# One chunk in each 12th and 13th group fetched row by row through SP, with other shares for DVE and ACT

## The chip, the cores and the metric

The kernel runs on one core of one Trainium2 chip. The core has five engines that run their own instruction streams: TensorE (PE; its weight loads are shown apart as PEld), VectorE (DVE), ScalarE (ACT), GpSimd (POOL) and SyncE (SP). They are held together by semaphores. Sixteen DMA engines move data between HBM and the on-chip memories; SP issues plain transfers, POOL issues the indirect ones (gathers). PSUM, the memory that PE writes to, is divided into banks. The metric is the time on the device in microseconds (us), as the median of several runs.

## The reference

The model is a layer norm, a two-layer graph network and a residual, over 12,500 nodes of 128 features and 200,000 edges that are sorted by their destination:

```python
h = jnp.maximum(_layernorm(x, axis=-1), 0.0)
deg = segment_sum(ones, dst);  wsum = segment_sum(edge_weight, dst)
w = edge_weight / jnp.maximum(wsum, EPS)[dst]
feat = relu(h @ W_pool + b_pool)
neigh = segment_max(feat[src] * w[:, None], dst)        # 0 where deg is 0
rst = h @ W1_self + neigh @ W1_neigh + b1
h1 = relu(rst / jnp.maximum(norm(rst), EPS))
neigh2 = segment_sum(h1[src] * w[:, None], dst) / jnp.maximum(deg, 1.0)[:, None]
out = x + relu(h1 @ W2_self + neigh2 @ W2_neigh + b2)
```

The costly parts are the two gathers, `feat[src]` and `h1[src]`: 200,000 rows of 512 bytes each, in random order.

## The kernel before

**Groups and chunks.** The edges are taken in 391 groups of 512 (`NG = 391`, `G = 512`); the last has 320. A group has four chunks `j = 0..3` of 128 edges. A gathered chunk is a tile of 128 partitions (edges) by 128 columns (features). Layer 1 goes over all groups with one Python loop over `i`, layer 2 with a second one. Both are written with a manual schedule: the order in which the loop body states the instructions is the order in which each engine runs them. The body of turn `i` works on several groups at once, each in another stage.

**Three ways to fetch a chunk.** Most chunks come by POOL: `gather` (L513) issues one indirect DMA per chunk (L520), which reads 128 rows of the table in HBM (`feat_d` in layer 1, `h_d` in layer 2). Some chunks are left out there (the argument `besides`) and fetched from a copy of the table that lies turned in SBUF (`one_way`, `other_way`: features on partitions, nodes along the columns), where a row is a column. The class `Columns` (L709) does this on DVE, two columns per instruction (`two_by_two`, L797, recorded as L800), or on ACT, one per instruction (`one_by_one`, L790, recorded as L788). For each such chunk SP loads the list of its 128 places (`listed<-at_d`, L738), the engine reads 16 of them at a time into registers (`TENSOR_LOAD`, L742), and copies 16 columns; these eight steps are spread over the turns ahead of the chunk's group. `every` says in each how many groups the engine takes a chunk, `j` says which chunk, `first` which group comes first.

**Layer 1** (loop at L1002; the first `FIRST = 16` groups are computed from `x` itself while the tables are made). Turn `i`: POOL gathers group `i` into a ring of buffers, which is 18 groups long at first and shrinks to 14 and to 8 (`buffer`, L134); ACT scales the four chunks of the group by their edge weights into `gs` (L1035); PE turns group `i-1` into PSUM, `pm` (L1040); DVE runs a segmented running maximum over `pm` (the scan, L1055), and two groups' worth of selection follows: `sel` (L1067, made by DVE, three buffers), `sc` (L1078, L1081), PE's transposes `pr` (L1095), ACT's copy `rows` (L1050), PE's products of `rows` and `sel` (L1104), and ACT's copy of the 48 result columns into the accumulator (L985). Nodes whose edges are all done go through the linear stage `nodes1` in five turns, among them a store of `h` to `h_d` (L886). A chunk from DVE or ACT holds a row of the normalised `x` in layer 1, so PE multiplies it by `W_pool` (L951) and ACT cuts it (L954) to make a row of `feat`.

**Layer 2** (loop at L1216). Turn `i`: POOL gathers group `i` into a ring of eight; DVE makes the weighted places of the group (L1165 and L1169, tile `s`), fetching some columns between the two; PE multiplies the four chunks of group `i-1` by `s` into `pa` (L1175, L1177; three buffers in PSUM); DVE adds `pa` of group `i-2` into the accumulator (L1180). A chunk fetched by columns is turned back by PE into `flip` (L1151, two halves of one tile in one PSUM bank) two turns ahead of its group, and copied into the ring by ACT (L1154, recorded as L788). `nodes2` makes the output rows.

**SP's queue.** SP runs its instructions in order. In layer 1 it loads four groups' keep masks at a time (`kt`, L602, into two buffers), the lists for the columns (L738), and the stores of `h` (L886). In layer 2 it loads lists, rows of `x` (L895), and stores the output (L915). A load that overwrites a buffer waits for that buffer's last reader, and what stands behind it in the queue waits with it.

**POOL's queue** holds almost nothing but the gathers. A gather waits until the ring buffer that it writes has been read: by ACT (L1035) in layer 1, by PE (L1177) in layer 2.

Of the kernel before, what the change touches and what calls it, by code (L numbers as in the profile page):

```python
# [41 lines left out]
TABLES_AT = (16512, 66880)  # L42
BURST = 16
HIGH = 1.0e30
KEPT = 4
# [4 lines left out]
def gnn_kernel(ctx, tc, x, src, dst, ew, w_pool, b_pool, w1s, w1n, b1, w2s, w2n, b2, out):  # L50
# [461 lines left out]

    def gather(gt, table_d, g, only=None, last=None, besides=()):  # L513

        t, r, ne, chunks = edges_of(g)
        limit = {} if last is None else dict(bounds_check=last, oob_is_err=False)
        for j, k in chunks if only is None else chunks[only:only + 1]:
            if any(c.j == j and c.takes(g) for c in besides):
                continue
            nc.gpsimd.indirect_dma_start(  # L520
                out=gt[:k, j, :], out_offset=None, in_=table_d[:, :],
                in_offset=bass.IndirectOffsetOnAxis(ap=srcT[:k, t, j, r:r + 1], axis=0), **limit)
        return gt
# [180 lines left out]
    def pairs_of(g):  # L704

        t, r, ne, _ = edges_of(g)
        return t, r, ne, [(j, min(P, ne // 2 - j * P)) for j in range(-(-ne // (2 * P)))]

    class Columns:  # L709
# [212 lines left out]
    with tc.manual_schedule(), tc.tile_pool(name="ew", bufs=3) as wk, \  # L922
# [15 lines left out]
        for k, engine, copy, j, every, first in (  # L938
                (0, mybir.EngineType.DVE, two_by_two, 1, 6, FIRST + 16),
                (1, mybir.EngineType.Activation, one_by_one, 3, 5.5, FIRST + 12)):  # L940

# [11 lines left out]
            def cut(g, _, k=k, rows_of_chunk=rows_of_chunk):  # L953
# [48 lines left out]
        for i in range(max(turn) + 6):  # L1002
# [11 lines left out]
            if FIRST <= i < NG:  # L1014
                gts[i] = gather(buffer(i, True), feat_d, i, besides=bycol)

# [106 lines left out]
            for c in bycol:  # L1123
                c.turn(i, c.multiplied)
        assert not busy
        i = NG
# [5 lines left out]
    with tc.manual_schedule(), tc.tile_pool(name="ew2", bufs=3) as wk, \  # L1132
            tc.tile_pool(name="ep2", bufs=2, space=PSUM) as ps:
        place = ps.tile([P, 2 * Q, CW], F32, bufs=1)
        hit, iota = place[:, :Q, :], place[:, Q:, :]
        flip = ps.tile([P, 2, P], F32, bufs=1)
        for j in range(Q):
# [5 lines left out]
        for k, engine, copy, j, every, first in (  # L1143
                (0, mybir.EngineType.DVE, two_by_two, 1, 3, 17),
                (1, mybir.EngineType.Activation, one_by_one, 2, 3.5, 12)):

# [3 lines left out]
            def turned(g, _, k=k, slot=slot):  # L1150
                nc.tensor.transpose(flip[:, k], slot(g), ident)  # L1151

            def back(g, _, k=k, slot=slot):
                by_scalar(slot(g), flip[:, k], **({} if k else {"scale": signs}))  # L1154
# [16 lines left out]
        def window_product(g):  # L1171
            chunks = edges_of(g)[3]
            pas[g] = ps.tile([P, LW], F32, name="pa", bufs=3)
            gt, s = gts.pop(g), ss.pop(g)
            nc.tensor.matmul(pas[g], ones_r[0:1, :P], nothing[0:1, :], start=True, stop=False)  # L1175
            for j, k in reversed(chunks):
                nc.tensor.matmul(pas[g][:, SHIFT[j]:SHIFT[j] + CW], gt[:k, j, :], s[:k, j, :], start=False, stop=j == 0)  # L1177

# [37 lines left out]
        for i in range(max(turn) + 2):  # L1216
            for c in bycol:
                c.turn(i, c.load)
            if EARLY <= i < NG:
                gts[i] = gather(buffer(i, False), h_d, i, besides=bycol)  # L1220
                weighted_places(i, lambda: bycol[0].fetch_one(i))
# [18 lines left out]
            if i == NG - 1:  # L1240
                for n in (HI - 2, HI - 1):
                    own[n] = flip[:, 0] if n % 2 else ps.tile([P, Q, D], F32, name="pl", bufs=1)[:, 0]
                    linear_own(own[n], n, "2s")
# [135 lines left out]
```

## Time and profile before

| | |
|---|---|
| median of 3 runs | 3544.11 us (3543.92 to 3545.5) |
| time of the profiled execution | 3545.64 us |
| its span, first to last instruction | 3543.9 us |
| layer 1's scans | 121 to 1844 us |
| layer 2's weighted places | 1871 to 3526 us |
| busy: DVE, ACT, POOL, PE | 3130.4, 3081.4, 2619.8, 2211.6 us |
| gathers by POOL in layer 1, in layer 2 | 1373, 1330 |
| instructions L788 on ACT, L800 on DVE | 21,376 columns and 233 copies; 11,840 pairs |
| SP: transfers issued in the column lists' line L738 | 359 |

How the lines of the profile are read: a row of the busiest groups gives line, engine, operation, `output<-inputs` and the count; behind the bar the time in which at least one of them ran and the mean duration in ns of one; behind the second bar the idle time of the engine just before them and what ended it. Where instructions overlap, as they do on DVE and ACT, the mean duration is longer than the time that each adds. "Issue" is idle time in which the engine waited for nothing that the profile shows. A row of waits says who waited (engine, tile, line), for whom, for how long in total, how often and the longest time. A timeline row begins with start and length in us; a last bracket holds the idle time ahead. A row of a stage table gives the stretch in us from the start, its length, and the busy time and count of the engine (of all engines in the order PE, PEld, DVE, ACT, POOL where there are five pairs), then the granted clock of PE, the share of the DMA engines and GB/s. A row of a line's instructions gives the duration in ns as minimum, median and maximum; engines with a `q` are their queues: register reads, semaphore waits and DMA issues, which are not counted as busy.

### The profile page before, as it was taken

To read this page: it belongs to the slowest core of one execution; us is meant where nothing else is said; L and a number is where in the kernel's file an instruction comes from. 1 tells how busy PE (TensorE), PEld (TensorE's weight loads), DVE (VectorE), ACT (ScalarE), POOL (GpSimd) and SP (SyncE) were. 2 spreads that over 40 slices of the span, in tenths; PEclk is the share of its full clock that TensorE was granted. 3 is DMA by queue.
4 is the path that set the end of the run, shared out by engine and by line. 5 is a ranking of instruction groups with operands and counts; after the bars stand their busy time and mean duration, and the time that the engine had idled before them with its cause. 6 is when DMAs were issued, how large, how long until landed. Compare 5 with 4: busy or idle time off the path is not lost.

```text
span 3543.9 us, 71968 instructions
## 1 busy us (share of the span) xinstructions
PE 2211.6 (62%) x9504; PEld 1920.0 (54%) x9504; DVE 3130.4 (88%) x16737; ACT 3081.4 (87%) x25633; POOL 2619.8 (74%) x2784
## 2 busy tenths in 40 slices
PE   7666666666666666566565667565565556556556
PEld 6455555555656555555554555555455555455545
DVE  7799999999999999998866888888888888888887
ACT  6689999999999999898967888888888888888885
POOL 6577777777777777777777777777777777777774
PEclk8665555555555555555555555555555555555555
DMA  6433332333333333332222222222222222222221
GB/s 223 130 97 90 94 88 83 88 86 88 86 87 86 88 86 88 86 88 86 83 82 54 54 60 75 60 63 63 60 60 63 63 60 62 63 59 59 62 62 49
DMA packets 132987, 280.13 MB, mean 79 GB/s; under 512 B 49446, under 2 KB 58764, under 8 KB 132494
## 3 DMA queue, kind: packets, MB, share of 16 engines
q0 software_dynamic: 88544, 181.42, 20.2%
q1 hardware_dynamic: 43214, 93.11, 7.8%
q14 instruction: 414, 3.39, 0.3%
q8 instruction: 79, 1.29, 0.2%
q10 hardware_dynamic: 736, 0.92, 0.1%
HBM read 253.41 MB, written 21.87 MB: 78 GB/s over the span
## 4 chain that ended last, share of the span: by engine, by line
DVE 49%; ACT 16%; issue 12%; POOL 6%; PE 6%; DVEq 5%; DMA 4%; ACTq 1%; POOLq 0%
DVE gt L800 25%; ACT gt L788 7%; POOL gt L520 6%; DVE pm L1055 6%; DVE picked L800 5%; DVEq L742 5%; ACT gs L1035 4%; DMA gt<-feat_d,srcT 3%; PE pa L1177 2%; DVE sel L1067 2%; DVE s L1169 2%; PE pf L625 2%; DVE sc L1078 2%; DVE place L1165 1%; ACT rows L1050 1%
## 5 line engine op out<-in xcount | busy, mean ns | idle before, releaser
L788 ACT ACTIVATE gt<-way 128x1 f32 x21376 | 2125.3, 189 | 226.8 <-PE pa L1177 164.5
L520 POOL DMA_INDIRECT gt<-h_d,srcT x1318 | 1246.1, 945 | 411.5 <-issue 340.8
L520 POOL DMA_INDIRECT gt<-feat_d,srcT x1192 | 1127.5, 946 | 369.2 <-issue 302.0
L800 DVE SCALAR_TENSOR_TENSOR gt<-b,way 128x2 f32<-128x2 f32 x8000 | 1155.1, 215 | 182.7 <-issue 154.3
L1177 PE MATMUL pa<-s,gt 128*128 128x24 f32 x3102 | 736.5, 390 | 535.0 <-DVE s L1169 462.4
L1177 PEld LDWEIGHTS pa<-s,gt 128*128 128x128 f32 x3102 | 690.6, 327 | 573.4 <-DVE s L1169 502.8
L1040 PE MATMUL pm<-ident,gs 128*128 128x128 f32 x1499 | 393.5, 415 | 257.9 <-ACT gs L1035 232.1
L800 DVE SCALAR_TENSOR_TENSOR picked<-b,way 128x2 f32<-128x2 f32 x3840 | 541.7, 211 | 1.9 <-issue 1.7
L1055 DVE TENSOR_TENSOR_SCAN pm<-kt,carry,pm 128x512 f32<-128x512 bf16 x389 | 496.3, 1276 | 46.0 <-PE pm L1040 45.8
L1035 ACT ACTIVATE gs<-gt,ewT 128x128 f32<-128x128 f32 x1303 | 414.9, 390 | 73.6 <-DMA gt<-feat_d,srcT 60.1
L1104 PEld LDWEIGHTS pn<-sel,rows 128*128 128x128 f32 x1564 | 354.3, 313 | 170.5 <-ACT way L985 73.2
L1040 PEld LDWEIGHTS pm<-ident,gs 128*128 128x128 f32 x1499 | 283.9, 221 | 294.3 <-ACT gs L1035 276.6
L1104 PE MATMUL pn<-sel,rows 128*128 128x48 f32 x1564 | 356.9, 374 | 135.1 <-ACT way L985 58.6
L1067 DVE TENSOR_SCALAR sel<-cols,lastT,invT 128x48 f32<-128x48 f32 x782 | 245.7, 314 | 0.0
L1095 PE MATMUL pr<-ident,sc 128*128 128x128 f32 x782 | 235.9, 403 | 3.4 <-DVE r_first L291 2.4
L1081 DVE COPY_PREDICATED sc<-kt,pm 128x256 f32<-128x256 int16 x389 | 167.1, 430 | 0.0
L1095 PEld LDWEIGHTS pr<-ident,sc 128*128 128x128 f32 x782 | 164.5, 220 | 4.2 <-ACT gs L1035 3.7
L1078 DVE COPY sc<-pm 128x256 f32<-128x256 f32 x391 | 159.7, 408 | 3.8 <-PE pr L1095 3.7
L1050 ACT ACTIVATE rows<-pr 128x256 f32<-128x256 f32 x392 | 142.1, 363 | 5.3 <-PE pn L1104 5.2
L851 PE MATMUL pn<-w_2n,way 128*128 128x128 f32 x192 | 79.2, 515 | 102.2 <-DVE way L1180 102.2
L1165 DVE TENSOR_TENSOR place<-place,locT 128x96 f32<-128x96 f32 x391 | 100.8, 258 | 46.1 <-DVE way L1180 32.2
L520 POOL DMA_INDIRECT w2T<-feat_d,srcT x96 | 90.8, 946 | 51.9 <-issue 24.1
(303 smaller groups left out, 2735.1 us busy)
## 6 DMA issues: line engine op xcount, KB each, us to landing
kt<-keep_d SPq DMA_DIRECT2D x97, 512.0 KB
gt<-h_d,srcT POOLq DMA_INDIRECT x1318
gt<-feat_d,srcT POOLq DMA_INDIRECT x1192
feat_d<-fr SPq DMA_DIRECT2D x24, 256.0 KB
xr<-in_x SPq DMA_DIRECT2D x24, 256.0 KB
out<-o SPq DMA_DIRECT2D x24, 256.0 KB
h_d<-h SPq DMA_DIRECT2D x47, 128.0 KB
listed<-at_d SPq DMA_DIRECT2D x359, 0.5 KB
```

Source lines behind the costliest of these rows:

```text
L520: nc.gpsimd.indirect_dma_start(out=gt[:k, j, :], out_offset=None, in_=table_d[:, :], in_offset=bass.IndirectOffsetOnAxis(ap=srcT[:k, t, j, ...
L788: nc.scalar.activation(out, in_, AF.Copy, **scale)
L800: nc.vector.scalar_tensor_tensor(slot[:, r + e:r + e + 2], zero_high, columns_read[e], columns_read[e + 1].to_broadcast([P, 2]), op0=OP.su ...
L1035: nc.scalar.activation(gss[i][:k, j, :], gt[:k, j, :], AF.Copy, scale=ewT[:k, t, j, r:r + 1])
L1040: nc.tensor.transpose(pms[i - 1][:, j * P:j * P + k], gs[:k, j, :], ident[:k, :k])
L1050: nc.scalar.activation(rws[g][:k, j, :], pr[:k, j, :], AF.Copy)
L1055: nc.vector.tensor_tensor_scan(pm[:, :ne], kt[:, :ne], pm[:, :ne], carry, op0=OP.add, op1=OP.max)
L1067: nc.vector.tensor_scalar(part, cols[:k, 1, :], lastT[:k, t, j, r:r + 1], invT[:k, t, j, r:r + 1], op0=OP.is_equal, op1=OP.mult)
L1078: nc.vector.tensor_copy(sc[:, :ne // 2], two[:, :, 1])
L1095: nc.tensor.transpose(prs[g][:k, j, :], sc[:, j * P:j * P + k], ident)
L1104: nc.tensor.matmul(pas[g], rows[:k, j, :], sel[:k, j, :], start=j == 0, stop=j == len(chunks) - 1)
L1177: nc.tensor.matmul(pas[g][:, SHIFT[j]:SHIFT[j] + CW], gt[:k, j, :], s[:k, j, :], start=False, stop=j == 0)
```

## The change

A third way to fetch a chunk is added, the class `Rows`: SP copies the 128 rows of a chunk one by one from the table in HBM into a tile `ga` (two buffers), 512 bytes each, with the source taken from a register. It takes chunk 0 of each 12th group in layer 1 (from group 40 to below group 383) and of each 13th in layer 2 (from 26 to below 390). `gather` leaves these chunks out.

For such a chunk SP loads the 128 source numbers from `src` (turn `g - every - 3`), DVE shifts them left by nine bits, which makes byte offsets of them (one turn later), and in eight steps spread over the turns `g - every - 1` to `g - 3` SP reads 16 of them into registers and issues 16 transfers. All 128 add to one semaphore of the chunk. In layer 1 ACT waits for it ahead of its last scaling instruction of the group, in layer 2 PE waits for it ahead of its last product.

Further: the shares of DVE and ACT are set anew (layer 1: DVE in each 6.5 groups instead of 6, ACT in each 6 instead of 5.5; layer 2: DVE in each 3.25 instead of 3, ACT in each 3.25 instead of 3.5). The two halves of `flip` become two tiles in a PSUM bank each; `pa` has two buffers instead of three, and `sel` in layer 1 has two instead of three. In layer 2's turn, the transposes `turned` are stated ahead of ACT's fetch and of the copies `back` instead of behind them. The lists lie in a second row of the tile that holds `bases`.

```diff
-    bases = const.tile([1, NT * P], I32)
+    bases_and_rows = const.tile([2 * 32, NT * P], I32)
+    bases, row_lists = bases_and_rows[0:1, :], bases_and_rows[32:33, :]
...
-            if any(c.j == j and c.takes(g) for c in besides):
+            if j == 0 and byrow and byrow.takes(g) or any(c.j == j and c.takes(g) for c in besides):
                 continue
...
+    class Rows:
+
+        def __init__(self, pool, table_d, every, first, end):
...
+            for g in range(first, end, every):
+                for s in range(P // BURST):
+                    turn = g - every - 1 + s * every // (P // BURST)
+                    self.plan.setdefault(turn, []).append((g, s * BURST))
...
+        def turn(self, i):
+            g = i + self.every + 3
+            if self.takes(g):
+                nc.sync.dma_start(self.list_of(g), src[None, g * G:g * G + P])
+            g = i + self.every + 2
+            if self.takes(g):
+                nc.vector.tensor_scalar(self.list_of(g), self.list_of(g), ROW_SHIFT, None, op0=OP.logical_shift_left)
+
+        def rows(self, i):
+            for g, r in self.plan.get(i, ()):
+                if g not in self.tiles:
+                    self.tiles[g] = self.pool.tile([P, D], F32, name="ga", bufs=2)
+                to = self.tiles[g].bitcast(U8)
+                _, at = nc.values_load_multi_w_load_instructions(
+                    self.list_of(g)[:, r:r + BURST], [mybir.EngineType.SP], min_val=0, max_val=(N - 1) << ROW_SHIFT,
...
+                for k in range(BURST):
+                    row = nc.sync.dma_start(to[r + k:r + k + 1, :], self.bytes[None, bass.ds(at[k], 4 * D)])
+                    row.then_inc(self.sem(g), 16)
...
+        def tile(self, g, engine):
+            n = (g - self.first) // self.every // len(self.sems) + 1
+            came = engine.wait_ge(self.sem(g), 16 * P * n)
...
-                (0, mybir.EngineType.DVE, two_by_two, 1, 6, FIRST + 16),
-                (1, mybir.EngineType.Activation, one_by_one, 3, 5.5, FIRST + 12)):
+                (0, mybir.EngineType.DVE, two_by_two, 1, 6.5, FIRST + 16),
+                (1, mybir.EngineType.Activation, one_by_one, 3, 6, FIRST + 12)):
...
+        byrow = Rows(wk, feat_d, 12, FIRST + 24, NG - 8)
...
-                    nc.scalar.activation(gss[i][:k, j, :], gt[:k, j, :], AF.Copy, scale=ewT[:k, t, j, r:r + 1])
+                    rows_j = byrow.tile(i, nc.scalar) if j == 0 and byrow.takes(i) else gt[:k, j, :]
+                    nc.scalar.activation(gss[i][:k, j, :], rows_j, AF.Copy, scale=ewT[:k, t, j, r:r + 1])
...
-                sel = sels[due(3)] = wk.tile([P, Q // 2, LW], F32, name="sel")
+                sel = sels[due(3)] = wk.tile([P, Q // 2, LW], F32, name="sel", bufs=2)
...
+            byrow.turn(i)
+            byrow.rows(i)
...
-        flip = ps.tile([P, 2, P], F32, bufs=1)
+        flips = [ps.tile([P, P], F32, name=f"flip{k}", bufs=1) for k in range(2)]
...
-                (0, mybir.EngineType.DVE, two_by_two, 1, 3, 17),
-                (1, mybir.EngineType.Activation, one_by_one, 2, 3.5, 12)):
+                (0, mybir.EngineType.DVE, two_by_two, 1, 3.25, 17),
+                (1, mybir.EngineType.Activation, one_by_one, 2, 3.25, 12)):
...
+        byrow = Rows(wk, h_d, 13, 26, NG - 1)
...
-            pas[g] = ps.tile([P, LW], F32, name="pa", bufs=3)
+            pas[g] = ps.tile([P, LW], F32, name="pa", bufs=2)
...
-                nc.tensor.matmul(pas[g][:, SHIFT[j]:SHIFT[j] + CW], gt[:k, j, :], s[:k, j, :], start=False, stop=j == 0)
+                rows_j = byrow.tile(g, nc.tensor) if j == 0 and byrow.takes(g) else gt[:k, j, :]
+                nc.tensor.matmul(pas[g][:, SHIFT[j]:SHIFT[j] + CW], rows_j, s[:k, j, :], start=False, stop=j == 0)
...
+            for c in bycol:
+                c.turn(i, c.turned)
             by_one.fetch_one(i)
             for c in bycol:
                 c.turn(i, c.back)
-            for c in bycol:
-                c.turn(i, c.turned)
             by_one.ahead()
             by_one.fetch_rest(i)
+            byrow.turn(i)
+            byrow.rows(i)
```

More of the change, by code (lines that the diff above doesn't have):

```diff
@@ L43 @@
 BURST = 16
+ROW_SHIFT = 9
 HIGH = 1.0e30
@@ L511, in edges_of, with gather @@
         return *divmod(g, P), ne, [(j, min(P, ne - j * P)) for j in range(-(-ne // P))]
-    def gather(gt, table_d, g, only=None, last=None, besides=()):
+    def gather(gt, table_d, g, only=None, last=None, besides=(), byrow=None):
         t, r, ne, chunks = edges_of(g)
@@ L707, in pairs_of, with takes, list_of, key @@
         return t, r, ne, [(j, min(P, ne // 2 - j * P)) for j in range(-(-ne // (2 * P)))]
+    class Rows:
+        def __init__(self, pool, table_d, every, first, end):
+            self.pool, self.every, self.first, self.end = pool, every, first, end
+            self.name = f"rows{every}"
+            self.sems = [tc.alloc_semaphore(f"{self.name}_{k}") for k in range(4)]
+            self.bytes = table_d[:, :].bitcast(U8).rearrange("n b -> (n b)")
+            self.tiles, self.plan = {}, {}
+            assert first > every + 4
+            for g in range(first, end, every):
+                for s in range(P // BURST):
+                    turn = g - every - 1 + s * every // (P // BURST)
+                    self.plan.setdefault(turn, []).append((g, s * BURST))
+        def takes(self, g):
+            return (g - self.first) % self.every == 0 and self.first <= g < self.end
+        def list_of(self, g):
+            k = (g - self.first) // self.every % 2 * P
+            return row_lists[:, k:k + P]
+        def turn(self, i):
[12 more added lines that the diff above has]
+                    self.list_of(g)[:, r:r + BURST], [mybir.EngineType.SP], min_val=0, max_val=(N - 1) << ROW_SHIFT,
+                    skip_runtime_bounds_check_because="sources of edges are nodes, as the gathers have it")
+                for k in range(BURST):
+                    row = nc.sync.dma_start(to[r + k:r + k + 1, :], self.bytes[None, bass.ds(at[k], 4 * D)])
+                    row.then_inc(self.sem(g), 16)
+                    tc.no_tile_sem_insts.add(row.ins.name)
+                    tc.add_to_no_dep_group(self.key(g), row.ins)
+        def key(self, g):
+            return f"{self.name}_{g}"
+        def sem(self, g):
+            return self.sems[(g - self.first) // self.every % len(self.sems)]
+        def tile(self, g, engine):
+            n = (g - self.first) // self.every // len(self.sems) + 1
+            came = engine.wait_ge(self.sem(g), 16 * P * n)
+            tc.declare_fence(came.ins, group=self.key(g))
+            return self.tiles.pop(g)
@@ L1014, in gnn_kernel @@
             if FIRST <= i < NG:
-                gts[i] = gather(buffer(i, True), feat_d, i, besides=bycol)
+                gts[i] = gather(buffer(i, True), feat_d, i, besides=bycol, byrow=byrow)
             if i < FIRST:
@@ L1150, in turned @@
             def turned(g, _, k=k, slot=slot):
-                nc.tensor.transpose(flip[:, k], slot(g), ident)
+                nc.tensor.transpose(flips[k], slot(g), ident)
             def back(g, _, k=k, slot=slot):
-                by_scalar(slot(g), flip[:, k], **({} if k else {"scale": signs}))
+                by_scalar(slot(g), flips[k], **({} if k else {"scale": signs}))
             bycol.append(Columns(engine, copy, None, other_way, 1, lists_of(k), slot,
@@ L1219, in gnn_kernel @@
             if EARLY <= i < NG:
-                gts[i] = gather(buffer(i, False), h_d, i, besides=bycol)
+                gts[i] = gather(buffer(i, False), h_d, i, besides=bycol, byrow=byrow)
                 weighted_places(i, lambda: bycol[0].fetch_one(i))
@@ L1241, in gnn_kernel @@
                 for n in (HI - 2, HI - 1):
-                    own[n] = flip[:, 0] if n % 2 else ps.tile([P, Q, D], F32, name="pl", bufs=1)[:, 0]
+                    own[n] = flips[0] if n % 2 else ps.tile([P, Q, D], F32, name="pl", bufs=1)[:, 0]
                     linear_own(own[n], n, "2s")
```

## The prediction

> **What bounds the kernel now.** I read the page first: its span, the busy shares, and the chain that ended last.
>
> ```profile
> span 3543.9 us, 71968 instructions
> ...
> PE 2211.6 (62%) x9504; PEld 1920.0 (54%) x9504; DVE 3130.4 (88%) x16737; ACT 3081.4 (87%) x25633; POOL 2619.8 (74%) x2784
> ...
> DVE 49%; ACT 16%; issue 12%; POOL 6%; PE 6%; DVEq 5%; DMA 4%; ACTq 1%; POOLq 0%
> ```
>
> By these lines DVE leads and POOL has a quarter of its time left. A stretch of POOL's timeline says otherwise:
>
> ```profile
> 2599.56 0.94 POOL L520 DMA_INDIRECT gt<-h_d,srcT  x1 [0.30 <-issue]
> 2600.80 0.94 POOL L520 DMA_INDIRECT gt<-h_d,srcT  x1 [0.30 <-issue]
> 2602.05 0.95 POOL L520 DMA_INDIRECT gt<-h_d,srcT  x1 [0.30 <-issue]
> ```
>
> A gather is shown busy for 0.94 us and the next follows after 0.30 us of its own issuing, so POOL spends 1.25 us on each and is full at a shown 76%. The stage tables come next. The first fence has all engines; then come POOL's gathers (L520), the scans (L1055, one per group of layer 1) and the weighted places (L1169, one per group of layer 2), in the same stretches; count in brackets.
>
> ```profile
> 240.00:1340.00 1100.00, 701.92 (x3188) 624.35 (x3188) 1076.18 (x4603) 1050.98 (x7756) 827.26 (x876) 0.55 0.31 88
> 1340.00:1840.00 500.00, 305.90 (x1353) 272.93 (x1352) 450.07 (x1947) 434.92 (x3208) 377.28 (x398) 0.53 0.30 84
> 2080.00:2780.00 700.00, 427.72 (x1759) 366.40 (x1759) 594.56 (x4031) 606.91 (x6015) 529.37 (x561) 0.50 0.24 63
> 2780.00:3480.00 700.00, 416.65 (x1731) 358.56 (x1730) 593.91 (x4032) 604.96 (x5992) 522.66 (x554) 0.50 0.23 61
> ```
> ```profile
> 240.00:1340.00 1100.00, 827.26 (x876) 0.55 0.31 88
> 1340.00:1840.00 500.00, 377.28 (x398) 0.53 0.30 84
> 2080.00:2780.00 700.00, 529.37 (x561) 0.50 0.24 63
> 2780.00:3480.00 700.00, 522.66 (x554) 0.50 0.23 61
> ```
> ```profile
> 240.00:1340.00 1100.00, 321.58 (x252) 0.55 0.31 88
> 1340.00:1840.00 500.00, 140.05 (x110) 0.53 0.30 84
> ```
> ```profile
> 2080.00:2780.00 700.00, 39.68 (x161) 0.50 0.24 63
> 2780.00:3480.00 700.00, 39.93 (x162) 0.50 0.23 61
> ```
>
> Layer 1 until 1340 us: a group takes 1100/252 = 4.365 us and DVE is busy 98% of it. A group needs 4 - 1/6 - 1/5.5 = 3.652 gathers, so 252 groups use up 920 while POOL issues 876: the store of chunks gathered ahead shrinks by 44. From 1340 on it is gone: 500/110 = 4.545 us a group, which is 3.652 x 1.25. POOL issues without a pause throughout, so its count of gathers sets the end of layer 1.
>
> Layer 2 needs 4 - 1/3 - 1/3.5 = 3.381 gathers a group, 544 for the 161 groups of the first half; POOL issues 561 and gains a lead of 17, until the ring of eight buffers is full. So POOL is not the bound there. A group takes 1400/323 = 4.334 us. The waits of DVE and ACT from 2080 to 3480:
>
> ```profile
> DVE gt L800 <- issue: 132.1, 457, 1.3
> DVE place L1165 <- DVE way L1180: 27.6, 71, 1.0
> ```
> ```profile
> ACT gt L788 <- PE pa L1177: 126.6, 55, 6.3
> ACT gt L788 <- issue: 32.9, 96, 0.8
> ACT gt L788 <- PE flip L1151: 21.6, 15, 3.1
> ```
>
> DVE is busy 1188.5 of 1400 us, and 160 us more are waits for its own list reads and results: 96%, with nobody else named. DVE bounds layer 2. ACT is busy 1211.9 us and waits 126.6 us for a ring buffer to be free, which is real slack: it is about 9% away from being the bound.
>
> **The change, part by part.** Counted from the two loops' bounds, layer 1 goes from 60 to 56 chunks by DVE and from 66 to 61 by ACT, and 29 come by SP: 20 gathers fewer. Layer 2 goes from 125 to 115 by DVE, from 108 to 117 by ACT, and 28 by SP: 27 gathers fewer. ACT thus fetches nine chunks more in layer 2 and four more in all. The prices of a chunk:
>
> ```profile
> L788 ACT ACTIVATE gt<-way 128x1 f32 x21376 | 2125.3, 189 | 226.8 <-PE pa L1177 164.5 <-issue 53.1 <-DMA gt<-h_d,srcT 1.5
> ...
> L800 DVE SCALAR_TENSOR_TENSOR gt<-b,way 128x2 f32<-128x2 f32 x8000 | 1155.1, 215 | 182.7 <-issue 154.3 <-PE pa L1177 5.4
> ...
> L800 DVE SCALAR_TENSOR_TENSOR picked<-b,way 128x2 f32<-128x2 f32 x3840 | 541.7, 211 | 1.9 <-issue 1.7
> ...
> L788 ACT ACTIVATE gt<-flip 128x128 f32<-128x128 f32 x108 | 28.0, 259 | 18.6 <-PE flip L1151 18.3
> ```
>
> These instructions overlap, so busy time over count is the price. ACT: 2125.3/21376 = 99.4 ns, 12.7 us for 128 columns, 13.3 us with the copy back and its issue gaps. DVE in layer 2: (1155.1 + 182.7)/125 = 10.7 us; in layer 1: 543.6/60 = 9.1 us.
>
> *Layer 1.* POOL: 20 x 1.25 = 25 us less. DVE: 4 x 9.1 = 36 us less, and 29 shifts of a list more, each on one partition, taken at the 0.21 us of a column pair: 6 us. ACT: 5 x 13 = 65 us less. Both give up more than POOL, so POOL keeps setting the end: -25 us. I keep back 5 us, because ACT now also waits for SP's tile, at a time when it has no lead to live on: **-20 us**, between -25 and 0.
>
> *Layer 2*, a group, in steady state. DVE: 4.334 - (1/3 - 1/3.25) x 10.7 = 4.06, with shifts 4.07 us. POOL: (52 - 4 - 4 - 1)/13 x 1.25 = 4.135 us. ACT: without the wait for PE pa it works 4.334 x (1 - 126.6/1400) = 3.94 us; added are (1/3.25 - 1/3.5) x 13.3 = 0.29 us: 4.23 us. If the wait for PE flip goes as well, since the two turned tiles then no longer share a bank, 0.07 us less: 4.16 us. So the bound passes from DVE to ACT, with POOL beside it. I take 4.20, the middle: (4.334 - 4.20) x 323 groups = **-43 us**. Bounds: POOL's 27 x 1.25 = 34 us plus about 15 us of lead that is used up, -49; and 0, should ACT lose its gain to waits.
>
> *Two pools made smaller.* `sel` goes from three to two buffers and `pa` likewise. With two `pa`, PE may begin group x only after DVE has added x-2, which stands a fetch of eight column pairs (8 x 0.144 = 1.2 us) behind the weighted places that PE waits for now; PE is busy 61% there and a group's product is needed two turns later: nothing. With two `sel`, DVE waits where PE's product of two groups before is late. What can make it late is PE's own wait:
>
> ```profile
> L1104 PEld LDWEIGHTS pn<-sel,rows 128*128 128x128 f32 x1564 | 354.3, 313 | 170.5 <-ACT way L985 73.2 <-DVE r L865 49.0 <-ACT way L890 46.2
> ```
>
> At most the 119 us held by ACT could reach DVE; below nothing is excluded, since a wait gives no time back. DVE has 36 - 6 us of new room and before the end of layer 1 the 50 us that it idles after 1340, so I take 0. The reordering of `turned` and `back` changes no engine's own order: 0.
>
> *SP's new work* is what decides. Each chunk is 8 list reads and 128 transfers of 512 bytes, in a queue that also issues `kt`, the columns' lists and the stores. Its prices:
>
> ```profile
> L738 SPq DMA_DIRECT2D listed<-at_d x359: 214/215/313, 198.6 to 3494.4; - x180
> ```
> ```profile
> L602 SPq DMA_DIRECT2D kt<-keep_d x98: 319/342/435, 117.8 to 1823.9; - x98
> ```
> ```profile
> 336.50 0.53 SPq L738 DMA_DIRECT2D listed<-at_d  x2
> ```
> ```profile
> L742 ACTq TENSOR_LOAD <-listed x1392: 1002/1019/1431, 206.6 to 3503.2; - x199
> ```
>
> The list transfer also moves one run of 512 bytes into one partition: 0.215 us, two of them in 0.53 us, so 0.265 each with the step to the next. A row's source comes from a register, which no row shows; it cannot be cheaper than 0.265. The upper bound is the largest form, `kt`, 0.342 + 0.05 = 0.39 us. I take 0.285, near the lower end, since size and shape are the list's. A read of 16 registers is 1.02 us on ACT; SP's is taken alike. A chunk costs SP 128 x 0.285 + 8 x 1.02 + about 3.2 for three `kt`, four lists and stores = 47.9 us in layer 1, and 48.0 in layer 2 (eight lists, no `kt`). There is room for 12 x 4.365 = 52.4 us and 13 x 4.20 = 54.6 us: SP would be 91% and 88% full, hidden. The covers end at 0.320 us a row in layer 1 and 0.337 in layer 2. Beyond, each 10 ns more costs 29 x 1.28 + 28 x 1.28 = 73 us, for SP is then the pace: ACT stands at the wait for SP's rows (in layer 2 PE), behind it the column fetches and window copies, and DVE stands at the shift of a list that SP sends late. On SP itself, `kt` and the columns' lists queue behind the rows. At 0.342 us a row the sum is -20 + 82 - 43 + 18 = +37 us; at 0.39 it is -20 + 260 - 43 + 190 = +387 us.
>
> [...]
>
> Transfers: 7,296 rows of 512 bytes are 3.7 MB beside 280 MB, with the transfer engines 23 to 31% busy: 0.
>
> **Sum.** -20 - 43 = -63 us against the profiled execution's 3545.6 us (span 3543.9 and 1.7 around it), 3482.6; the median of the runs is 1.5 us below that execution, so **3482 us** is forecast.
>
> **Rivals.**
> *SP has no time for it* (slower). For it: the room is 35 ns a row, and SP is in order; it loses its lead at each wait:
>
> ```profile
> SPq L738 <- DVEq L742: 1202.0, 141, 14.4
> SPq L602 <- DVE r L865: 659.8, 44, 17.9
> ```
>
> Against it: the same rows show SP long idle ahead of the others, and a row is planned three turns before its use. It decides from 0.337 us a row (sum zero). At 0.342 us: 3581 us; at 0.39: 3931 us; at twice the list's duration, 0.43 us, over 4200 us, to which I give 0.03 of this case's chance. [...]
> *The smaller pools give DVE waits* in layer 1: about half of the 119 us arrives, more than DVE's new room, and layer 1 gains nothing; PE delayed in layer 2 takes 10 us more: 3482 + 20 + 10 = 3512 us. For it: layer 1 runs DVE at 98%. Against it: ACT gives up 65 us there, and PE waits for ACT.
> *ACT spoils layer 2*: at 4.33 us a group, full and with every remaining wait on the path, layer 2 stays as it is: 3525 us. For it: 4.23 of 4.334 us is 98%. Against it: its waits are a ring's, and shrink as it falls behind.
> That the edit does not do what it says is excluded: the instruction order has 47 gathers, 896 column pairs on DVE and the matching lists less, and 512 columns on ACT more.
>
> **Chances and range.** My forecast 0.52; SP short 0.30; smaller pools 0.09; ACT 0.09. Within 0.2% (7 us, about what a measurement of this kernel can tell from no change) fall 0.02 of SP's case and 0.02 of the pools'; slower 0.28 of SP's and 0.01 of the pools'. That leaves faster 0.67, same 0.04, slower 0.29. The fast cases lie from 3470 (-25 and -49) to 3537 and hold 0.67; with the same ones and SP up to 0.35 us a row (+95, 3640) it is 0.8. So the range is 3466 to 3640; my forecast's own is 3466 to 3505.
>
> **What would show it.** POOL's gathers: 2,720 instead of 2,767 and still 1.25 us apart in layer 1. SP: rows 0.29 us apart, in bursts of 16, SP waiting for DVE between them. In layer 2 about 4.2 us a group, ACT without its wait for PE pa, POOL's lead not growing. The prediction is wrong if a row takes over 0.32 us start to start, if ACT or PE is seen waiting for SP's rows, or DVE at the shift or at `sel`.

## The result and the profile after

The changed kernel is slower. It takes 3654.6 us (median of four runs, 3652.3 to 3656.2) against 3544.3 us of the kernel before, a ratio of 1.031 with a 95% interval of 1.0295 to 1.0321. The forecast was 3482 us, range 3466 to 3640. The profiled execution took 3653.2 us, span 3651.5.

The page of the changed kernel: its span, the busy shares, and the chain that ended last by engine.

```profile
span 3651.5 us, 86331 instructions
...
PE 2204.4 (60%) x9476; PEld 1922.3 (53%) x9476; DVE 3024.5 (83%) x15898; ACT 3124.8 (86%) x26135; POOL 2573.3 (70%) x2737
...
DVE 37%; SPq 28%; issue 10%; ACT 8%; DVEq 5%; PE 5%; DMA 4%; POOL 2%; ACTq 1%; POOLq 0%
```

DVE's work fell by 106 us, as meant, and yet the span grew. What is new is SPq, SyncE's queue: it wasn't in the chain of before, and now holds 28% of it. The same stretches by stage, all engines first (columns as in the prediction), then the scans of layer 1 (L1114) and the weighted places of layer 2 (L1231):

```profile
240.00:1340.00 1100.00, 665.86 (x2964) 594.79 (x2964) 989.96 (x4108) 941.47 (x6808) 779.16 (x826) 0.52 0.28 83
...
2140.00:2840.00 700.00, 415.21 (x1723) 359.08 (x1724) 544.81 (x3676) 634.64 (x6332) 510.85 (x542) 0.50 0.22 63
```
```profile
240.00:1340.00 1100.00, 300.87 (x236) 0.52 0.28 83
```
```profile
2140.00:2840.00 700.00, 39.27 (x159) 0.50 0.22 63
```

In layer 1 DVE goes from 98% to 90% busy, and POOL from 876 gathers to 826; in layer 2 ACT is the busiest, with 91%. None of the five sets the pace: at 1.25 us a gather POOL has work for 94% of the first stretch and 97% of the second. A group takes 1100/236 = 4.66 us (before 4.365), so twelve groups take 55.9 us. In layer 2 a group takes 700/159 = 4.40 us (before 4.334), thirteen 57.2 us. Both are about the same length: that of one chunk of rows on SyncE. What SyncE does there, by its timeline (start, length, what):

```profile
1000.41 5.09 SPq L749 DMA_DIRECT2D ga<-feat_d  x16
1005.55 0.37 SPq L943 DMA_DIRECT2D h_d<-h  x1
1006.01 0.23 SPq L795 DMA_DIRECT2D listed<-at_d  x1
1006.35 0.34 SPq L604 DMA_DIRECT2D kt<-keep_d  x1
1006.78 0.23 SPq L795 DMA_DIRECT2D listed<-at_d  x1
1008.40 5.16 SPq L749 DMA_DIRECT2D ga<-feat_d  x16
1013.91 0.23 SPq L735 DMA_DIRECT2D bases_and_rows<-in_src  x1
1015.53 11.57 SPq L749 DMA_DIRECT2D ga<-feat_d  x32
1027.22 0.35 SPq L604 DMA_DIRECT2D kt<-keep_d  x1
```

It works almost without a break: the gaps of 1.3 to 1.4 us ahead of each burst are register reads, which this view leaves out, and from 300 to 1300 us all other gaps over 0.1 us add up to 9.5 us. The two lines by themselves (shortest, median and longest in ns):

```profile
L749 SPq MOVE ga<-feat_d x3712: 29/29/38, 229.3 to 1868.0; - x196
L749 SPq DMA_DIRECT2D ga<-feat_d x3712: 224/228/307, 229.4 to 1868.1; - x196
...
L745 SPq TENSOR_LOAD <-bases_and_rows x456: 973/1232/1797, 228.1 to 3582.2; - x152
```

So a row is two instructions, a MOVE of the register and the transfer: 16 in 5.09 us, 0.32 us from one to the next, and 0.332 us in the mean of all from 300 to 1300 us. A read takes 1.24 us in the mean and 1.30 with the step to the next. A chunk needs 128 x 0.332 + 8 x 1.30 + 3.2 (the prediction's figure for the rest) = 56.1 us. SyncE's waits were 1202.0 and 659.8 us in the prediction's two rows; here the largest for the same two issues (lists and `kt`) are:

```profile
SPq L795 <- ACTq L799: 27.7, 13, 24.1
SPq L604 <- DVE r L922: 27.7, 3, 14.3
```

The others stand behind it. Of the lists for the columns, the view of their line in SyncE's queue (L795) says who waited for them, for how long in us and how often. Before, nobody waited for them (L738); now it is 307 us in all:

```profile
who waited for it (us, times):
  DVE s L1231: 132.2, 27
  ACT gs L1094: 62.3, 15
  DVE picked L857: 43.6, 12
  ACT gt L845: 42.4, 8
  DVE sel L1126: 26.4, 6
```

The view of all waits has the first of these rows as "issue" (132.2 us too). It also has ACT waiting for the rows, and DVE at the shift:

```profile
ACT gs L1094 <- ACTq L762: 36.4, 26, 2.5
...
DVE bases_and_rows L738 <- DMA bases_and_rows<-in_src: 33.8, 15, 5.4
```

### The profile page after: what moved, and what is told of

Read it like the earlier page. It is cut to its first block, busy times and chain, and to the rows that moved or that the text cites. A ratio compares the mean times of both kernels' runs of the same rounds, so it can differ in the third digit from the quotient of the medians.

```text
span 3651.5 us, 86331 instructions
## 1 busy us (share of the span) xinstructions
PE 2204.4 (60%) x9476; PEld 1922.3 (53%) x9476; DVE 3024.5 (83%) x15898; ACT 3124.8 (86%) x26135; POOL 2573.3 (70%) x2737
## 4 chain that ended last, share of the span: by engine, by line
DVE 37%; SPq 28%; issue 10%; ACT 8%; DVEq 5%; PE 5%; DMA 4%; POOL 2%; ACTq 1%; POOLq 0%
SPq L749 21%; DVE picked L857 8%; DVE pm L1114 8%; DVE gt L857 7%; ACT gt L845 6%; SPq L745 6%; DVEq L799 5%; DVE sel L1126 3%; DVE sc L1137 2%; DMA listed<-at_d 2%; DVE sc L1140 2%; POOL gt L522 2%; PE pf L627 1%; ACTq L799 1%; PE pa L1240 1%
## 5 line engine op out<-in xcount | busy, mean ns | idle before, releaser
L845 ACT ACTIVATE gt<-way 128x1 f32 x22016 | 2187.9, 189 | 63.3 <-PE pa L1240 27.6
L522 POOL DMA_INDIRECT gt<-h_d,srcT x1291 | 1219.7, 945 | 465.8 <-issue 316.5
L522 POOL DMA_INDIRECT gt<-feat_d,srcT x1171 | 1106.7, 945 | 450.1 <-issue 300.8
L857 DVE SCALAR_TENSOR_TENSOR gt<-b,way 128x2 f32<-128x2 f32 x7360 | 1060.9, 215 | 165.9 <-issue 128.3
L1240 PEld LDWEIGHTS pa<-s,gt 128*128 128x128 f32 x3046 | 681.2, 327 | 614.6 <-issue 498.7
L857 DVE SCALAR_TENSOR_TENSOR picked<-b,way 128x2 f32<-128x2 f32 x3584 | 507.0, 212 | 63.3 <-issue 63.1
L1094 ACT ACTIVATE gs<-gt,ewT 128x128 f32<-128x128 f32 x1276 | 407.3, 390 | 142.3 <-issue 68.6
L1114 DVE TENSOR_TENSOR_SCAN pm<-kt,carry,pm 128x512 f32<-128x512 bf16 x389 | 496.2, 1276 | 4.4 <-DMA kt<-keep_d 2.4
L1237 PE MATMUL pa<-nothing,ones_r 1*128 1x48 bf16 x391 | 78.9, 202 | 513.2 <-DVE way L1243 506.0
L1231 DVE TENSOR_TENSOR s<-place,w2T 128x96 f32<-128x96 f32 x391 | 97.0, 248 | 134.3 <-issue 132.2
```

The source lines that it names most:

```text
L522: nc.gpsimd.indirect_dma_start(out=gt[:k, j, :], out_offset=None, in_=table_d[:, :], in_offset=bass.IndirectOffsetOnAxis(ap=srcT[:k, t, j, ...
L845: nc.scalar.activation(out, in_, AF.Copy, **scale)
L857: nc.vector.scalar_tensor_tensor(slot[:, r + e:r + e + 2], zero_high, columns_read[e], columns_read[e + 1].to_broadcast([P, 2]), op0=OP.su ...
L1094: nc.scalar.activation(gss[i][:k, j, :], rows_j, AF.Copy, scale=ewT[:k, t, j, r:r + 1])
L1114: nc.vector.tensor_tensor_scan(pm[:, :ne], kt[:, :ne], pm[:, :ne], carry, op0=OP.add, op1=OP.max)
L1240: nc.tensor.matmul(pas[g][:, SHIFT[j]:SHIFT[j] + CW], rows_j, s[:k, j, :], start=False, stop=j == 0)
```

## The experiments

Call SyncE's time for one chunk of rows its need, and the time of the groups among which one such chunk falls its room (in layer 1 twelve groups). Theory A: the need exceeds the room and is the pace. Theory B: something else in the change, the smaller pools above all, costs the time. On some chips the kernel before itself takes about 5000 us instead of 3544 us, so every run is compared only with the kernel before on its own chip; e8 to e10, e17 and e18 ran where it takes 3545 us, all others where it takes about 5000 us.

### The first seven, where the kernel before takes 5000 us

```diff
 e1, e5: every 14th and 15th group
-byrow = Rows(wk, feat_d, 12, FIRST + 24, NG - 8)
+byrow = Rows(wk, feat_d, 14, FIRST + 24, NG - 8)
-byrow = Rows(wk, h_d, 13, 26, NG - 1)
+byrow = Rows(wk, h_d, 15, 26, NG - 1)
 e2: no rows, old shares (6 and 5.5 in layer 1, 3 and 3.5 in layer 2)
+byrow = Rows(wk, feat_d, 12, NG, NG)
+byrow = Rows(wk, h_d, 13, NG, NG)
 e3: no register reads, rows from fixed places
-self.bytes[None, bass.ds(at[k], 4 * D)]
+self.bytes[None, 4 * D * (r + k):4 * D * (r + k + 1)]
 e4: one transfer for two rows
+for k in range(0, BURST, 2): dma_start(to[r + k:r + k + 2, :], ...bass.ds(at[k], 8 * D)...)
 e6: the changed kernel itself
 e7: every 20th and 21st group
```

> SP takes a chunk in each 14th group of layer 1 and each 15th of layer 2, all else as in the changed kernel. Theory A (SP's own time is the pace: 128 rows of 0.332 us, 8 register reads of 1.30 us and 3.2 us of other transfers, 56.1 us a chunk): 14 groups of 4.38 us and 15 of 4.22 us leave 61 and 63 us, so SP is hidden and the time falls from 3654 to about 3490 us (3475 to 3510), with POOL's gathers 1.25 us apart in layer 1. Theory B (the pools with two buffers, or ACT's share in layer 2, hold the kernel up, and SP is only slow beside them): the time stays above 3600 us.

> No rows by SP and the shares of DVE and ACT of the kernel before; what is left of the change is sel and pa with two buffers, the two turned tiles in a bank each, and the transposes stated earlier. Theory A: the same as before within 0.3% (3535 to 3555 us). Theory B: 30 to 110 us slower than before, with DVE waiting at sel or PE's delay behind pa passed on.

> The changed kernel with SP's rows taken from fixed places (rows 0 to 127 of the table) and without the register reads, so the fetched chunk is the wrong one. Theory A: a row costs what the lists' transfer did, about 0.27 us, no read of 1.30 us stands between the bursts, a chunk is 38 us on SP and hidden: about 3482 us (3470 to 3500), the time that the prediction gave. Theory B: above 3600 us.

> The changed kernel with half as many transfers by SP: each moves two neighbouring rows of the table (1,024 bytes), so every second row of the chunk is the wrong one; the register reads stay. Theory A: 64 x 0.34 + 10.4 + 3.2 = 35 us a chunk, hidden: about 3485 us (3470 to 3500). If instead the register reads alone held SP up (8 of 1.30 us in a row of waits), it stays above 3560 us. Theory B: above 3600 us.

> The kernel with SP's chunk in each 14th and 15th group once more. In the first series ACT lost over 1,100 us to issuing its own instructions on that chip, in the kernel before as in all others (before took 5002 us there), so that nothing of SP's pace could be read from the times. On a chip where the kernel before takes about 3544 us, theory A gives 3490 us (3475 to 3510), theory B above 3600 us.

> The changed kernel itself on the experiments' chip, beside the kernel before. There a burst of 16 rows takes SP about 9 us instead of 5.1, and the kernel with SP's chunk in each 14th and 15th group is 3.4% slower than before. Theory A (SP's own time is the pace): the time goes with SP's number of chunks, 57 against 50, so 57/50 of the time that 50 chunks take, less what the other engines hold up beside: 5500 to 5850 us. Theory B (another part of the change is the cause): within 2% of the 5170 us of the kernel with 50 chunks.

> SP takes a chunk in each 20th group of layer 1 and each 21st of layer 2 (35 chunks). On the experiments' chip 20 groups take about 120 us and a chunk costs SP about 90 us, so theory A has SP hidden: within 1% of the 4990 to 5017 us of the kernels with cheaper rows, that is at the time of the kernel before. On a chip where the kernel before takes 3544 us: about 3495 us. Theory B: 3% slower than before or more, as with 50 chunks.

Measured, with the end of layer 1 (last scan) and the time from there to the last weighted places:

| kernel | us | ratio, 95% interval | layer 1 ends | layer 2 |
|---|---|---|---|---|
| e1 | 5175.5 | 1.034 [1.0319, 1.0361] | 2581 | 2574 |
| e5 (as e1) | 5167.2 | 1.0345 [1.0322, 1.0369] | | |
| e2 | 5038.0 | 1.0076 [1.0050, 1.0102] | 2528 | 2491 |
| e3 | 5017.1 | 1.003 [1.0017, 1.0042] | 2487 | 2508 |
| e4 | 4991.8 | 0.9978 [0.9967, 0.9988] | 2487 | 2484 |
| e6 | 5347.1 | 1.0686 [1.0650, 1.0722] | 2760 | 2562 |
| e7 | 5068.9 | 1.0121 [1.0081, 1.0160] | 2507 | 2549 |

Most of the expectations were for paces that don't hold there, and missed: e1 isn't hidden, e2 is 0.8% slower than the kernel before instead of the same within 0.3%, e6 lies between its two ranges, e7 is 1% above its own. SyncE's timeline of e6 shows part of why: the same 16 rows take 5.7 to 11.8 us in this stretch.

```profile
1005.18 11.83 SPq L749 DMA_DIRECT2D ga<-feat_d  x16
...
1018.80 19.09 SPq L749 DMA_DIRECT2D ga<-feat_d  x32
...
1040.35 5.69 SPq L749 DMA_DIRECT2D ga<-feat_d  x16
```

The engines lose time in the same way. In e2, ACT's column copies wait 1344.5 us for nothing but their own issue:

```profile
ACT gt L845 <- issue: 1344.5, 2261, 1.9
PEld pa L1240 <- ACT gt L845: 1192.2, 168, 16.7
```

ACT thus bounds layer 2 there, and the nine chunks more that the change gives it can bring no gain. What still follows: theory B is worth 0.8% there (e2, interval 0.5 to 1.0%), and the end of layer 1 moves with SyncE's load: 2760, 2581 and 2507 us with 29, 25 and 18 chunks of register rows, and 2487 us with 29 cheaper ones, 40 us before e2. This is for A. Layer 2 doesn't follow the load there: it takes 2562 us with 28 chunks of register rows (e6), 2574 with 25 (e1) and 2549 with 18 (e7), against 2491 with none (e2). Why stays open. Whether the engines' gain exists where the forecast was made, these runs can't say.

### e8, e9 and e10: the same two kernels where the kernel before takes 3545 us

e8 is the kernel of e1, e9 that of e3, e10 the kernel before.

> The same kernel as in e1: rows in each 14th group of layer 1 and each 15th of layer 2, all else as changed. Theory A (SyncE's own time for the rows is the pace of the changed kernel): a chunk needs 56.1 us of SyncE by the changed kernel's rows, the room is 14 x 4.37 = 61 us and 15 x 4.20 = 63 us, so the engines' gain comes back: 3480 to 3510 us where the kernel before takes 3544 us. Where the kernel before takes about 5000 us, as in e1, 5165 to 5180 us again. Theory B (the smaller pools, the separate turned tiles or ScalarE's larger share make it slower): 3560 us or more where the kernel before takes 3544 us.

> The same kernel as in e3: all rows of the change are fetched, but from fixed places, without register reads (the output is that of other rows). Theory A: a chunk then needs 128 x 0.301 + 3.2 = 41.7 us of SyncE, room 52.4 and 54.6 us, so 3475 to 3500 us where the kernel before takes 3544 us, and about 5015 us where it takes 5000 us. Theory B: as slow as the changed kernel, 3620 us or more, where the kernel before takes 3544 us.

> The kernel before itself, for its profile on the chip of these runs. If it takes about 5000 us there, ScalarE's steps of issue should be the longest idle entry of its waits, with some 0.7 us for instructions that take 0.1 us to start in the profile at 3544 us; the two layers would end near 2520 and 5000 us. If it takes 3544 us, the profile is that of before.

e8 took 3478.6 us, 0.9815 [0.9799, 0.9831]; e9 3467.2 us, 0.978 [0.9764, 0.9797]; e10 3543.4 us. Theory B is out there: both keep the smaller pools, the separate turned tiles and ScalarE's larger share, and gain 67 and 78 us. e8, which fetches the rows of its own lists, is faster than the kernel before and the changed one. In e9 the row is one instruction:

```profile
L746 SPq DMA_DIRECT2D ga<-feat_d x3712: 214/252/391, 215.3 to 1748.1; - x196
```

With the step to the next it is 0.299 us (mean of 2,346 steps), so a register adds 33 ns, though the transfer with a register is the shorter one (228 ns): the MOVE and the steps around it are what is added.

### e11 to e16: where the edge lies, and the reads alone

```diff
 e11, e14: every 13th and 14th group
 e12, e15: register reads kept, rows from fixed places as in e3
 e13, e16: the kernel of e2
```

> Rows in each 13th group of layer 1 and each 14th of layer 2, all else as changed. SyncE's need is 56.1 us a chunk by the changed kernel's rows; by the pace of e8 the room is 13 x 4.36 = 56.7 us and 14 x 4.13 = 57.8 us. Theory A (SyncE's time sets the pace where it exceeds the room): just covered, so within 20 us of e8: 3470 to 3500 us where the kernel before takes 3544 us. Theory B (what decides is something that grows with the rows, such as their transfers' load on memory): halfway between e8 and the changed kernel, near 3570 us. Where the kernel before takes about 5000 us, 5200 to 5300 us.

> As changed, with the register reads, but each row's transfer from a fixed place (the output is that of other rows): the reads' price without the registers' in the rows. SyncE's need: 128 x 0.299 + 8 x 1.30 + 3.2 = 51.9 us, room 12 x 4.33 = 52.0 us in layer 1 and 13 x 4.13 = 53.7 us in layer 2. Theory A: just covered, 3467 to 3490 us where the kernel before takes 3544 us, so that the 30 ns a row of the register form decide by themselves. If the reads decide instead (they delay more than their own time), 3550 us or more. Where the kernel before takes about 5000 us, 5050 to 5250 us.

> The kernel of e2: no rows by SyncE, the old shares of VectorE and ScalarE, with the smaller pools (two sel, two pa), the separate turned tiles and their order as changed. The prediction put these at 0 to 28 us: 3544 to 3555 us where the kernel before takes 3544 us. The rival of the smaller pools would have some 28 us more, 3570 us. Where the kernel before takes about 5000 us, 5038 us as in e2.

> The kernel of e11, for a chip where the kernel before takes 3544 us: need 56.1 us a chunk, room 56.7 us in layer 1 and 57.8 us in layer 2 by the paces of e8. Theory A: just covered, 3470 to 3500 us; theory B (a load that grows with the rows): near 3570 us. Where the kernel before takes about 5000 us, 5258 us again.

> The kernel of e12 (register reads kept, rows from fixed places, so the output is that of other rows), for a chip where the kernel before takes 3544 us: need 51.9 us a chunk, room 52.0 us in layer 1 and 53.7 us in layer 2. Theory A: just covered, 3467 to 3490 us, so that the 30 ns a row of the register form decide; if the reads decide by more than their own time, 3550 us or more. Where the kernel before takes about 5000 us, 5041 us again.

> The kernel of e2 and e13 (no rows by SyncE, old shares, smaller pools and separate turned tiles as changed), for a chip where the kernel before takes 3544 us: 3544 to 3555 us by the prediction's price for these parts; the rival of the smaller pools would have 3570 us. Where the kernel before takes about 5000 us, 5038 us again.

All six fell on chips with 5000 us: e11 5258.0 us, 1.0513 [1.0496, 1.0531], and e14 5253.8; e12 5040.7, 1.008 [1.0063, 1.0097], and e15 5043.8; e13 5038.2, 1.0076 [1.0058, 1.0093], and e16 5044.8. e11 stands in order of SyncE's load: its layer 1, with 27 chunks of register rows, ends at 2641 us, between e1's and e6's. Every 13th and 14th group stays untried where the kernel before takes 3545 us. e12 and e15 don't hold what they were meant to hold. In e17, where one of each 16 registers is used, all 456 reads are in the trace; in e12 none is used, and of the line of the reads only semaphore events are left, no TENSOR_LOAD:

```profile
L745 SPq EVENT_SEMAPHORE  x456: 3/17/783, 329.6 to 4926.9; - x152
```

But for these events SyncE issues what it does in e3, so they tell nothing of the reads; they took some 25 us longer than e3, and why stays open.

### e17 and e18: the reads without the registers, the registers without the reads

```diff
 e17: one row of each 16 uses its register
+place = 4 * D * (r + k)
+source = self.bytes[None, place:place + 4 * D] if k else self.bytes[None, bass.ds(at[k], 4 * D)]
 e18: one read a chunk
+if r == 0:
+    _, self.at = nc.values_load_multi_w_load_instructions(...)
-bass.ds(at[k], 4 * D)
+bass.ds(self.at[k], 4 * D)
```

> As changed, but 15 rows of each 16 come from fixed places, one by its register, so that the register reads stay (the output is that of other rows). SyncE's need where the kernel before takes 3544 us: 8 x (0.327 + 15 x 0.299) + 8 x 1.30 + 3.2 = 52.1 us, room 52.0 us in layer 1 and 53.7 us in layer 2 at the paces of e9. If the rows' register form decides: 3467 to 3490 us, e9's time or little over it; if the reads do: 3550 us or more. Where the kernel before takes about 5000 us (rows 0.54 us by register and 0.376 us fixed, reads 1.13 us in e11 and e12), need 63.5 us against 12 x 5.85 = 70 us in layer 1: 5015 to 5050 us if the rows' form decides, 5150 us or more if the reads do.

> As changed, but one register read for a chunk instead of eight: all its rows take their sources from the first 16 (the output is that of other rows). Need where the kernel before takes 3544 us: 128 x 0.332 + 1.3 + 3.2 = 47.0 us, covered by 52.0 us: 3467 to 3480 us either way, since both prices together made 56.1 us. Where the kernel before takes about 5000 us: 128 x 0.541 + 1.1 + 5 = 75 us against 70 us in layer 1, 83 us in layer 2: 5130 to 5200 us if the rows' form decides, 5015 to 5050 us if the reads do.

Where the kernel before takes 3545 us, e17 took 3481.2 us, 0.9818 [0.9802, 0.9835], and e18 3467.4 us, 0.9778 [0.9762, 0.9794]. The reads are there in e17, and gone but for one in eight in e18:

```profile
L745 SPq TENSOR_LOAD <-bases_and_rows x456: 977/1227/1887, 226.6 to 3405.9; - x152
```
```profile
L746 SPq TENSOR_LOAD <-bases_and_rows x57: 979/1136/1806, 229.3 to 3338.1; - x57
```

Together with e9 and the changed kernel, that is nearly each price alone, neither and both. The need is of one chunk on SyncE:

| rows | reads | need, us | time, us |
|---|---|---|---|
| fixed, 0.299 us | none (e9) | 128 x 0.299 + 3.2 = 41.5 | 3467.2 |
| register, 0.332 us | one (e18) | 42.5 + 1.3 + 3.2 = 47.0 | 3467.4 |
| 120 fixed, 8 register | eight (e17) | 38.5 + 10.4 + 3.2 = 52.1 | 3481.2 |
| register | eight (as changed) | 42.5 + 10.4 + 3.2 = 56.1 | 3654.6 |

Between 41.5 and 47.0 us nothing happens; at 52.1 the first 14 us are lost, and 4 us of need later 173 more. Which rows are fetched is not what differs: e9, e17 and e18 fetch other rows than the lists name (e18 the same 16 for a whole chunk), but with a register a transfer occupies SyncE as long in e18 as in the changed kernel (228 ns in the median), and e8 gains with the right rows.

```profile
L750 SPq DMA_DIRECT2D ga<-feat_d x3712: 224/228/647, 230.6 to 1748.1; - x196
```

The edge is the room, and e18's trace has it (columns as above: all engines, then L1115 and L1232):

```profile
240.00:1340.00 1100.00, 715.23 (x3194) 638.76 (x3193) 1070.98 (x4464) 1011.31 (x7328) 821.87 (x871) 0.53 0.31 89
...
2140.00:2840.00 700.00, 427.46 (x1805) 371.55 (x1805) 587.67 (x3964) 682.70 (x6816) 528.89 (x561) 0.50 0.24 64
```
```profile
240.00:1340.00 1100.00, 326.26 (x255) 0.53 0.31 89
```
```profile
2140.00:2840.00 700.00, 42.57 (x170) 0.50 0.24 64
```

With SyncE out of the way a group takes 1100/255 = 4.31 us in layer 1 and 700/170 = 4.12 in layer 2. The room is 12 x 4.31 = 51.8 us and 13 x 4.12 = 53.5 us. The changed kernel's need is 4.3 and 2.6 us over it, 29 and 28 times: 125 + 73 = 198 us, where 3654.6 - 3467.4 = 187 us was measured. By layer the rule is less exact: the changed kernel loses 100 us against e18 in layer 1, where the rule has 125, and 88 in layer 2, where it has 73. e17 leans the same way: 5 us in layer 1, where the rule has 9, and 9 in layer 2, where it has none. What makes layer 2 lose more stays open. SyncE has time to spare in e18, by the largest of its waits in the loops:

```profile
SPq L746 <- DVE place L1228: 116.8, 24, 16.9
```

## Why the prediction was wrong

The case named as the first rival, "SP has no time for it", is what happened. Step by step:

**Layer 1, -20 us: right where SyncE keeps up.** The last scan starts at 1843.6 us before and 1823.6 us in e18, where SyncE is out of the way:

```profile
L1115 DVE TENSOR_TENSOR_SCAN pm<-kt,carry,pm x389: 882/1280/1299, 131.9 to 1823.6; 128x512 f32<-128x512 bf16 x194, 128x320 f32<-128x320 bf16 x1
```

That it is 20 and not the 25 of POOL's count is in part luck, though: the 5 us were kept back for ACT waiting for SyncE's rows, and e18 has no such wait. What grew there, by 9 us, are POOL's own pauses between gathers (steps of over 1.3 us between 240 and 1830 us exceed 1.26 us by 15.6 us in all, before by 6.2).

**Layer 2, -43 us: the right direction, and too small.** From the last scan to the last weighted places it took 1681.6 us before, 1620.3 in e18: -61 us, beyond the prediction's own bound of -49. The forecast took ACT's pace, 4.20 us a group, the middle of 4.16 to 4.23; measured is 4.12. POOL issues 561 gathers in 700 us, 1.25 us each, and is full, at the 4.135 that the same paragraph has for it; that pace by itself is (4.334 - 4.135) x 323 = 64 us, so the bound of -49 didn't agree with it. In e18 PE waits long for POOL's gathered rows, which before it hardly did (first e18, then before):

```profile
PEld pa L1241 <- DMA gt<-h_d,srcT: 585.6, 324, 3.7
```
```profile
PEld pa L1177 <- DMA gt<-h_d,srcT: 4.9, 3, 2.1
```

ACT is 98% busy there (682.7 of 700 us) and keeps POOL's pace. So the bound passed to POOL with ACT beside it, not the other way round, and 4.23 us was too much for ACT.

**Smaller pools 0, turned tiles 0 to 0.07 us a group: no cost to be seen.** e18 has them and reaches layer 1's -20 us in full. They weren't run alone where the kernel before takes 3545 us. Where it takes about 5000 us they did cost something, 0.8 to 0.9% in three runs (e2, e13, e16); which of them, and why, stays open.

**SyncE's 47.9 us a chunk: the step that failed.** Two terms of it were too small. "I take 0.285, near the lower end, since size and shape are the list's": measured 0.332. Of the 47 ns, 33 are the register's (e9 against the changed kernel) and 14 are there with fixed places too: such a row's transfer takes 252 ns in the median where a list's took 215. "A read of 16 registers is 1.02 us on ACT; SP's is taken alike": measured 1.30 with its step. The rows add 6.0 us to the need and the reads 2.2. The room was also too large, since it was reckoned with layer 1's pace of before and 4.20 in layer 2: 52.4 and 54.6 us instead of 51.8 and 53.5.

Put into the prediction's own sum, the rows' price alone gives a need of 53.9 us, 2.1 and 0.4 us over the measured room: 72 us, and with the gain of 78 us a time just under the kernel before. The reads' price alone gives 50.1 us, hidden. It takes both to be slower, and e17 and e18 show the same thing from the other side: without either the loss is gone. The rule for beyond the edge, one microsecond a chunk for every microsecond short, held within 6% in all, with misses in both layers that partly cancel (100 us for 125, 88 for 73).

**"The covers end at 0.320 us a row in layer 1 and 0.337 in layer 2"** was where to look. With reads at 1.30 and the measured room these are (51.8 - 10.4 - 3.2)/128 = 0.298 and 0.312 us. The named bounds of a row, 0.265 to 0.39, had both edges well inside, and 0.332 is nearly their middle, 0.328. To set 0.285 was to settle by likeness what no row decided.

**What would show it** named the signs rightly: a row over 0.32 us start to start, ACT waiting for SyncE's rows (36.4 us), DVE at the shift (33.8). The largest was not among the signs, though the text has these lists queue behind the rows: DVE and ACT at late column lists (307 us).

## What to carry to other kernels

Work given to an idle queue has a budget, what it needs in a turn against the turn's length after the gain, and here the cost was next to nothing up to it (0.2 us between needs of 41.5 and 47.0 us) and about the whole excess in each turn beyond (187 us measured at 56.1 us, where the excess adds up to 198). When the bounds of a price include the edge, the nearest look-alike doesn't settle the forecast; count the instructions that a form issues (here a register source brought a MOVE of 29 ns of its own) before taking another form's row. Here the remedy was a slightly thinner load: every 14th and 15th group instead of the 12th and 13th turns 3654.6 us into 3478.6.

## What the runs showed of the hardware

Where the kernel before takes about 3545 us, a transfer of 512 bytes on SyncE took 0.299 us from a fixed place and 0.332 us from a register's, start to start: the MOVE of 29 ns and the steps around it, while the transfer itself is shorter (228 against 252 ns). SyncE's read of 16 registers took 1.23 us in the median beside ACT's 1.02. In e12 and e15, where no instruction uses the registers, the line of the reads has no TENSOR_LOAD; in e17, where one of each 16 is used, it has 456.

The same kernel took 3545 us on some chips and about 5000 on others. On the latter, ACT's column copies wait for their own issue for 1344.5 us in e2, and 16 rows on SyncE take 5.7 to 11.8 us in the stretch shown of e6 instead of 5.1. What makes their issue slow stays open.
